# Moving layer-0 loads of a fused convolution kernel from the convolution stretches into the expansion stretches

## The chip, the cores and the metric

The program runs on one core of a Trainium2 chip. The metric is the device time of one execution in microseconds (us); for the kernel before it is the median of three runs.

A core has a tensor engine (PE; its weight loads are listed apart as PEld), a vector engine (DVE), a scalar engine (ACT), GpSimd (POOL) and a sync engine (SP). Here SP issues nearly all loads and POOL all stores. The transfers themselves run on 16 DMA engines which all issuing engines share. Each engine runs its own instructions strictly in order, and the engines wait for one another through semaphores.

## The reference, cut to what matters

Four residual layers work on x of shape (4, 64, 256, 256) in float32. The change touches layer 0 alone:

```python
# layer 0, C = 64 channels, hidden = 192, patch p = 8
v = group_norm(x)                                  # 32 groups over the whole image
v = einsum('bchw,oc->bohw', v, w_in)               # 64 -> 384 channels, "expansion"
v = irfft2(rfft2(patches 8x8 of v) * fft_filter)   # per channel, per patch
v = depthwise_conv3x3(v, w_dw)                     # padding 1
x1, x2 = split(v, 2, axis=1)
x = x + einsum('bchw,oc->bohw', gelu(x1) * x2, w_out)   # "projection"
# layer 1: x + conv3x3(group_norm(x)); layer 2: x + a thresholded convolution;
# layer 3: x + a Fourier operator with 16x16 modes
```

The filter on a patch and the 3x3 convolution together are one linear map from the pixels of a patch and its neighbours to the pixels of a patch, with other weights for each of the 384 channels. The kernel builds these maps at its start and writes them to HBM as `wts`.

## The kernel before, in words

**Blocks.** Layer 0 is cut into 12 blocks p: three for each of the 4 images, each of 11 rows of patches (`NR`), with one row more on top. In a block the hidden channels are done in four groups (`kb` = 0 to 3). For each group there is first an *expansion stretch*: `expand(p, kb, t)` for the rows t = 0 to 11 that lie in the image. PE multiplies the normalized x row `xn` with `win` (L444 for even t, L450 for odd t), and ACT and DVE copy the result from PSUM into the large tile `u` (L459, L461 to L463). Then there is a *convolution stretch*: `convolve(p, kb, g)` for g = 0 to 11, in which PE applies the maps of four channel pairs (L494, L503), ACT does the gelu (L510), DVE multiplies by the gate (L511), and POOL stores the gated planes `g` to HBM (L514).

**Projection, one block late.** The gated planes of block p-1 are read back from HBM while block p is computed. `project(p-1, r, half)` takes the pixel rows r = 0 to 7 of all patches in two halves, 16 units in a block and four in each group. PE multiplies by `w_out` (L591, L598), DVE adds to the residual rows `r` and takes statistics (L607 to L618), and POOL stores the new x (L622). Before it, `load_half` must have loaded the residual rows (`load_r`, L559, two transfers, in half 0 only) and the gated planes (`load_g`, L546 and L550, six transfers in half 0 and eight in half 1). The tiles `g1` and `g6` have two buffers each, so the load for unit (r+1, half) waits for PE to be done with unit (r, half).

**Other loads.** `load_w` brings the maps for two convolutions, three loads ahead, into four buffers (L471). `load_stats` and `next_stats` read a tenth or so of the next image in each block (`st`, L627) and take its statistics on DVE (L320). `load_x` and `normalize_x` bring the rows of x for the next block (L418) and normalize them on ACT (L256) during kb 3. `st` and x share four buffers of the pool `p_x`.

**What sets the order.** The order of the instructions of PE, DVE, ACT and SP is the order in which the Python code writes them (`tc.manual_schedule`). POOL is placed by its data alone. A transfer issued by SP has a place in SP's list, but no time: SP issues it as soon as the instructions ahead of it in that list are issued and its own waits are over. These are the wait for a free buffer, the wait for data in HBM, and the wait for one of eight completion semaphores, which the transfers of SP use in turn, so that each waits for the one eight before it.

## Time and profile before

| what | value |
|---|---|
| median of 3 runs | 6649.44 us (6638.31 to 6666.61) |
| the profiled execution | 6626.21 us |
| its span | 6624.4 us |
| PE busy in the span | 6040.5 us (91%) |
| DVE, ACT, POOL busy | 4275.7, 3238.8, 1050.4 us |
| layer 0, from the first expansion to the end of the last convolution | about 100 to 3937 us of the span |
| loads by SP in the whole program | 923.09 MB, 54.8% of the time of 16 DMA engines |
| stores by POOL | 500.14 MB, 21.7% |
| instruction fetches, queue q8 | 843 transfers, 13.81 MB |

A row of waits reads: engine and tile that waited, "<-", what ended the wait, then the sum in us, the number of waits and the longest. "issue" means that the profile shows nothing for which the engine waited. A row of a window reads: from and to in us, busy us of PE, PEld, DVE, ACT and POOL with the number of instructions, the granted clock of PE (1.00 is full), the mean busy share of the 16 DMA engines (which may exceed 1 a little, as records of neighbouring packets overlap), and GB/s. A row of the timeline reads: start, duration, engine, line, operation, tiles, and in square brackets the idle time before it with its releaser.

### The profile page before, as it was taken

To read this page: it belongs to the slowest core of one execution; us is meant where nothing else is said; L and a number is where in the kernel's file an instruction comes from. 1 tells how busy PE (TensorE), PEld (TensorE's weight loads), DVE (VectorE), ACT (ScalarE), POOL (GpSimd) and SP (SyncE) were. 2 spreads that over 40 slices of the span, in tenths; PEclk is the share of its full clock that TensorE was granted. 3 is DMA by queue.
4 is the path that set the end of the run, shared out by engine and by line. 5 is a ranking of instruction groups with operands and counts; after the bars stand their busy time and mean duration, and the time that the engine had idled before them with its cause. 6 is when DMAs were issued, how large, how long until landed. Compare 5 with 4: busy or idle time off the path is not lost.

```text
span 6624.4 us, 238282 instructions
## 1 busy us (share of the span) xinstructions
PE 6040.5 (91%) x106712; PEld 3213.7 (49%) x106712; DVE 4275.7 (65%) x5924; ACT 3238.8 (49%) x4564; POOL 1050.4 (16%) x1646
## 2 busy tenths in 40 slices
PE   2999999999999999999999986999899999999987
PEld 1455555555555555555555543333344444443576
DVE  5556555555555555555555545999798898885355
ACT  4454434344434444344444422777777887783211
POOL 3111111111111111111111111111022222221011
PEclk9999999999999999999999997999999999999855
DMA  8577777777878877877767669999666666677889
GB/s 236 152 206 211 216 213 222 218 216 213 230 213 238 219 222 207 223 214 220 210 193 206 188 194 247 232 229 228 165 177 176 168 180 173 173 187 264 318 351 394
DMA packets 878510, 1447.67 MB, mean 219 GB/s; under 512 B 77252, under 2 KB 586452, under 8 KB 875444
## 3 DMA queue, kind: packets, MB, share of 16 engines
q1 hardware_dynamic: 725284, 923.09, 54.8%
q0 software_dynamic: 148672, 500.14, 21.7%
q8 instruction: 843, 13.81, 0.9%
q10 hardware_dynamic: 3536, 9.20, 0.5%
q14 instruction: 175, 1.43, 0.1%
HBM read 932.08 MB, written 500.04 MB: 216 GB/s over the span
## 4 chain that ended last, share of the span: by engine, by line
PE 82%; DMA 6%; ACT 5%; DVE 3%; issue 3%; SPq 0%; POOL 0%; ACTq 0%; DVEq 0%; POOLq 0%
PE pc L503 18%; PE pc L494 12%; PE m L869 10%; PE psu L444 9%; PE one L1110 8%; PE div L1069 6%; PE po L591 4%; ACT u L459 4%; PE psu L450 4%; PE psz L1099 2%; PE po L598 2%; DMA x<-x 2%; PE psa L1297 2%; DMA g<-g 2%; PE psy L1444 1%
## 5 line engine op out<-in xcount | busy, mean ns | idle before, releaser
L511 DVE TENSOR_TENSOR h<-h,pc 128x374 f32<-128x374 f32 x1152 | 574.7, 541 | 1268.7 <-ACT h L510 1267.7
L510 ACT ACTIVATE h<-pc 128x374 f32<-128x374 f32 x1152 | 492.6, 480 | 1824.9 <-PE pc L503 1822.0
L503 PE MATMUL pc<-u,w 64*16 64x374 f32 (+2 forms) x27648 | 1244.1, 483 | 0.0
L494 PE MATMUL pc<-u,w 64*64 64x374 f32 x9216 | 928.6, 494 | 81.1 <-DVE u L463 32.2
L514 POOL DMA_DIRECT2D g<-h x576 | 416.7, 723 | 3111.0 <-DVE h L511 2904.7
L503 PEld LDWEIGHTS pc<-u,w 64*16 64x16 f32 (+2 forms) x27648 | 413.8, 92 | 769.5 <-issue 768.9
L444 PE MATMUL psu<-win,xn 64*128 64x96 f32 x8704 | 627.0, 283 | 131.8 <-ACT u L459 110.5
L459 DVE COPY u<-psu 64x384 f32<-64x384 f32 x1088 | 604.3, 555 | 167.7 <-PE psu L444 155.7
L459 ACT COPY u<-psu 64x384 f32<-64x384 f32 x1088 | 560.0, 515 | 238.9 <-PE psu L444 218.8
L444 PEld LDWEIGHTS psu<-win,xn 64*128 64x128 f32 x8704 | 574.0, 192 | 202.6 <-ACT u L459 143.6
L1055 DVE TENSOR_TENSOR q<-xn 128x2313 f32<-128x2313 f32 (+2 forms) x256 | 627.4, 2492 | 1.7 <-ACT xn L256 1.7
L1110 PE MATMUL one<-z,wp 32*32 32x512 f32 x16384 | 592.1, 596 | 17.8 <-issue 13.6
L494 PEld LDWEIGHTS pc<-u,w 64*64 64x64 f32 x9216 | 350.3, 133 | 531.0 <-issue 354.7
L256 ACT ACTIVATE xn<-x,nb,r 128x1024 f32<-128x1024 f32 (+3 forms) x272 | 486.8, 1793 | 244.6 <-DMA x<-x 140.8
L1056 ACT ACTIVATE q<-q 128x2313 f32<-128x2313 f32 (+2 forms) x256 | 529.0, 2086 | 32.7 <-DVE q L1055 31.2
L450 PE MATMUL psu<-win,xn 64*64 64x96 f32 x17408 | 458.2, 252 | 81.9 <-issue 57.2
L1069 PE MATMUL div<-q,ones 64*32 64x512 f32 x8192 | 466.3, 594 | 12.9 <-ACT q L1056 9.3
L1110 PEld LDWEIGHTS one<-z,wp 32*32 32x32 f32 x16384 | 367.6, 103 | 223.6 <-issue 80.1
L450 PEld LDWEIGHTS psu<-win,xn 64*64 64x64 f32 x17408 | 395.5, 137 | 126.0 <-issue 77.0
L1143 POOL DMA_DIRECT2D x<-r x512 | 275.5, 547 | 969.8 <-DVE r L1140 945.1
L591 PE MATMUL po<-g,wo 128*64 128x176 f32 (+1 forms) x3072 | 315.8, 348 | 63.3 <-DMA g<-g 41.3
L869 PE MATMUL m<-t,wk 64*64 64x512 f32 x3072 | 341.1, 588 | 0.0
(162 smaller groups left out, 6668.1 us busy)
## 6 DMA issues: line engine op xcount, KB each, us to landing
g<-h POOLq DMA_DIRECT2D x576, 374.0 KB, 7.0
x<-x SPq DMA_DIRECT2D x240, 640.0 KB, 6.4
w<-wt SPq DMA_DIRECT2D x288, 448.0 KB, 8.4
x<-x SPq DMA_DIRECT2D x100, 1024.0 KB, 14.2
g<-g SPq DMA_DIRECT2D x414, 187.0 KB, 5.7
g<-g SPq DMA_DIRECT2D x736, 93.5 KB, 6.0
x<-in_x_dram SPq DMA_DIRECT2D x256, 256.0 KB, 8.1
x<-o POOLq DMA_DIRECT2D x128, 512.0 KB, 8.2
```

The source lines that it names most:

```text
L444: nc.tensor.matmul(ps[s][:, k, at], xn[halves[s], n : n + 2].rearrange("p n r w -> p (n r w)"), win[halves[s], kb, 0 : 2 * PB], start=True ...
L450: nc.tensor.matmul(ps[s][halves[1 - odd], k, at], xn[halves[s], n + odd].rearrange("p r w -> p (r w)"), win[halves[s], kb, PB * (1 - odd) ...
L459: copy(at(h, 8 * s + o), v[k, c : c + PB])
L494: nc.tensor.matmul(out(C * c, C, k, h), w[halves[h], k, 2 * (G % 2) + c, 0:C], cells(h, 4 * g + 2 * k + c, 0, 0), start=True, stop=False, ...
L503: nc.tensor.matmul(out(q, m, k, h), w[halves[h], k, 2 * (G % 2) + c, c0 : c0 + m], cells(h, 4 * g + 2 * k + c, down, right), start=False, ...
L511: nc.vector.tensor_mul(h[:, k], h[:, k], ps[k][:, 1, 0:L])
L591: nc.tensor.matmul(out(k, s, x), wo1, moving(g1[:, 2 * k], 2 * half + k, s, x), start=(x == 0), stop=False, skip_group_check=True,)
L869: nc.tensor.matmul(rows2(m)[halves[j], s], w[dx][halves[s]], ts[n][halves[s], i, 2 * j : 2 * j + 2, dx : dx + W], start=(dx == 0), stop=(d ...
L1055: nc.vector.tensor_sub(d, p0, p1)
L1056: nc.scalar.activation(d, d, AF.Square)
L1069: ins = nc.tensor.matmul(ps[quarters[j], h], ones[halves[h]], q[n, g, k][halves[h], r + 2 * j : r + 2 * j + 2, o : o + W], start=(m == 0), ...
L1110: ins = nc.tensor.matmul(rows2(ps[g])[quarters[j], k], w[quarters[i]], z[quarters[i], h, 2 * j + dy : 2 * j + dy + 2, dx : dx + W], tile_p ...
```

## The change

Three things are done, all in layer 0.

1. The maps are stored in HBM, and held in the tile `w`, with the two halves k of a channel next to each other. A load of `w` then reads one run of 3584 bytes per partition, where it read two of 1792 bytes.
2. `unit` (projection and the next load) stands at g = 0, 3, 6, 9, where it stood at 1, 4, 7, 10. The loads that follow the projections at g = 6 and 9, and the first two of a block, are kept in a list `later` and written at t = 7 and t = 9 of the next expansion stretch.
3. The statistics parts (kb 0 to 2) and the first four x rows of the next block (kb 3) are written at t = 8, 9, 10 and 11 of the expansion stretch. They stood at g = 0, 3, 6, 9, and at g = 11 of kb 2. `next_stats` runs at the odd g.

```diff
-        wts = [dr.tile([2, 64, 2, Q, NC], F32, name=f"wt{t}") for t in range(HID // C)]
+        wts = [dr.tile([2, 64, Q, 2, NC], F32, name=f"wt{t}") for t in range(HID // C)]
...
-            w = wl[j] = p_w.tile([128, 2, 4, NC], F32, tag="w", name=f"w_{j}")
+            w = wl[j] = p_w.tile([128, 4, 2, NC], F32, tag="w", name=f"w_{j}")
             nc.sync.dma_start(
-                w, wts[k // 8][:, :, :, 4 * (k % 8) : 4 * (k % 8) + 4].rearrange("h i k c n -> (h i) k c n")
+                w, wts[k // 8][:, :, 4 * (k % 8) : 4 * (k % 8) + 4].rearrange("h i c k n -> (h i) c k n")
             )
...
             for p in range(NB + 1):
-                ahead = 1
+                ahead, later = 1, []
...
                 for r in range(ahead):
                     for half in range(2):
-                        load_half(p - 1, r, half)
-
-                def unit():
+                        later.append((p - 1, r, half))
+                        if p == NB:
+                            load_half(*later.pop())
+
+                def unit(wait=False):
                     at = next(units, None)
                     if at:
                         project(p - 1, *at)
-                        load_half(p - 1, at[0] + ahead, at[1])
+                        later.append((p - 1, at[0] + ahead, at[1]))
+                        if not wait:
+                            load_half(*later.pop(0))
...
                     for t in range(NR + 1):
                         if 0 <= i0 + t < NP:
                             expand(p, kb, t)
+                        if t in (7, 9) and later:
+                            load_half(*later.pop(0))
+                        if t >= 8:
+                            if kb == 3 and t - 8 < len(fresh):
+                                load_x(fresh[t - 8])
+                            elif kb < 3 and nk:
+                                loaded.append(nk.pop(0))
+                                load_stats(b + 1, loaded[-1])
...
-                        if g in (1, 4, 7, 10):
-                            unit()
+                        if g in (0, 3, 6, 9):
+                            unit(wait=g > 3)
                         if kb < 3:
-                            if g % 3 == 0:
-                                if len(loaded) == 2 or not nk:
-                                    for k in loaded[: 1 if nk else 2]:
-                                        next_stats(b + 1, loaded.pop(0))
-                                if nk:
-                                    k = nk.pop(0)
-                                    load_stats(b + 1, k)
-                                    loaded.append(k)
-                            if kb == 2 and g == NG - 1:
-                                for row in fresh[:4]:
-                                    load_x(row)
+                            if g % 2 and loaded:
+                                next_stats(b + 1, loaded.pop(0))
```

The remaining lines of the diff give the matmuls of `convolve` and the stores of `weights` the new order of the indices. The numbers of instructions on PE, DVE and SP don't change.

More of the change, by code (lines that the diff above doesn't have):

```diff
@@ L395, in weights @@
                             nc.gpsimd.dma_start(
-                                wts[t][h, 32 * hh : 32 * hh + 32, k, :, n0 : n0 + n].rearrange("i c n -> c i n"),
+                                wts[t][h, 32 * hh : 32 * hh + 32, :, k, n0 : n0 + n].rearrange("i c n -> c i n"),
                                 T[quarters[2 * h + k], :, :, c0 : c0 + n].rearrange("p a b n -> p (a b) n"),
@@ L494, in convolve @@
                         nc.tensor.matmul(
-                            out(C * c, C, k, h), w[halves[h], k, 2 * (G % 2) + c, 0:C], cells(h, 4 * g + 2 * k + c, 0, 0),
+                            out(C * c, C, k, h), w[halves[h], 2 * (G % 2) + c, k, 0:C], cells(h, 4 * g + 2 * k + c, 0, 0),
                             start=True, stop=False, tile_position=(h * C, c * C), skip_group_check=True,
@@ L503, in convolve @@
                             nc.tensor.matmul(
-                                out(q, m, k, h), w[halves[h], k, 2 * (G % 2) + c, c0 : c0 + m],
+                                out(q, m, k, h), w[halves[h], 2 * (G % 2) + c, k, c0 : c0 + m],
                                 cells(h, 4 * g + 2 * k + c, down, right),
```

## The prediction

> **What bounds the kernel now.** I read the page first. Its busy row and its slices put PE at 91% of the span, and at 90% or more in nearly every slice of layer 0 (slices 1 to 23), while the 16 DMA engines are busy 70 to 80% there.
>
> ```profile
> span 6624.4 us, 238282 instructions
> ...
> PE 6040.5 (91%) x106712; PEld 3213.7 (49%) x106712; DVE 4275.7 (65%) x5924; ACT 3238.8 (49%) x4564; POOL 1050.4 (16%) x1646
> ...
> PE   2999999999999999999999986999899999999987
> ...
> DMA  8577777777878877877767669999666666677889
> ```
>
> So a transfer matters only where PE ends up waiting. I asked for PE's waits from 300 to 3700 us:
>
> ```profile
> PE psu L444 <- ACT u L459: 94.3, 145, 1.5
> PE psu L450 <- issue: 57.2, 48, 4.2
> PE pc L494 <- DVE u L463: 29.3, 29, 1.3
> ...
> PE psu L444 <- issue: 18.7, 23, 1.8
> ...
> PE po L591 <- DVE h L511: 0.3, 1, 0.3
> ```
>
> No wait here ends with a landing of g, w, st or x (the 41.3 us of `po` waiting for g in the whole program lie in the drain after layer 0). The rest is eviction of `psu`, and 76 us of "issue", all in the expansion stretches. I took those apart in the timeline:
>
> ```profile
> 1700.59 0.40 PE L450 MATMUL psu<-win,xn 64*64 64x96 f32 x8 [2.28 <-issue]
> ```
>
> In the DMA records an instruction fetch of q8 runs from 1698.29 to 1699.34, and PE goes on 1.25 us later. The other long gaps from 1525 to 1720 us look alike: a fetch ends at 1530.34, the gap at 1531.55; 1626.38 and 1627.79. There are 843 fetches for 215,917 PE and PEld instructions: one per 256. A fetch starts late when SP has transfers in flight: by my count 1.8 us after the earliest point with none in flight, 4.5 us with six. An expansion stretch uses 256 instructions in 5.8 us (192 per pair of rows of 4.4 us), a convolution stretch in 7.1 us (128 per 3.53 us), so only the former starves. The windows show which stretches are loaded (first and second half of an expansion, of the convolution after it, then an expansion of kb 3):
>
> ```profile
> 1525.90:1540.10 14.20, 12.53 (x295) 11.50 (x288) 10.41 (x19) 9.61 (x19) 0.72 (x1) 0.88 0.87 277
> 1540.10:1554.20 14.10, 11.43 (x289) 10.29 (x289) 12.08 (x23) 11.34 (x23) 0.00 (x0) 1.00 0.30 53
> 1554.20:1581.30 27.10, 26.14 (x412) 10.94 (x420) 12.03 (x22) 5.75 (x13) 3.63 (x5) 0.94 0.54 143
> 1581.30:1608.30 27.00, 27.00 (x498) 11.39 (x482) 15.48 (x27) 5.14 (x12) 7.27 (x10) 1.00 1.05 292
> ...
> 1608.30:1622.70 14.40, 12.63 (x312) 11.62 (x310) 12.14 (x23) 11.36 (x23) 0.72 (x1) 1.00 1.02 286
> 1622.70:1637.20 14.50, 12.07 (x273) 10.91 (x271) 10.55 (x19) 9.51 (x19) 0.00 (x0) 0.88 0.85 146
> ```
>
> The DMA engines are full in the second half of the convolution and spill into the first half of the expansion; in kb 3 the x rows fill the second half too. Clock 0.88 is a stretch at half clock just after a stall.
>
> Measured from the timeline, an undisturbed expansion takes 23.6 us (first block of an image), 26.4 or 26.2 us (second, third). Above that, over blocks 1 to 11, stand 10.1 us in kb 0, 20.0 in kb 1, 15.1 in kb 2 and 32.0 in kb 3: 77 us. Convolution stretches have 31 us above their quiet lengths (52.5, 51.7, 53.3 us), mostly 1.6 us at their head at half clock. These 108 us (1.6%) are all that the placing of transfers can give back.
>
> **The Trainium skill.** "Runtime: NRT & Kernel Launch", Instruction fetch mechanics, says that instructions stream in blocks of 16 KiB (256 instructions) over the sequencer's own DMA queue and calls the cost mostly hidden. The block size agrees (13.81 MB in 843); hidden it is not, by 76 us. "DMA: Bandwidth & Descriptors", Issuing engines are not separate DMA queues, says all issuers share 16 engines; the late fetches agree. Its section Why small descriptors are slow gives about 3 cycles per packet besides 32 bytes a cycle. "TensorE: Matmul & The Clock Gate", What's actually happening, says that PE falls to half clock after an idle window of about 3.4 us. Here half clock lasts 3 to 7 us, but after gaps of only 1 to 2 us.
>
> **The change part by part.** *Weight runs.* 288 loads take 128 packets in place of 256. A 1792-byte packet takes 75 ns in the median; 3584 bytes are not in the trace, 4096 take 159 to 189, so no gain per byte shows. By the skill's price it is 59 against 57.5 cycles, 2.5% of 12% of DMA time. Nobody waits for w: 0 us. The weights lie in the same partitions in runs of 64 columns, so loads into PE cost the same.
>
> *Projections at g = 0, 3, 6, 9.* The same instructions, 2.05 us of PE each. At g = 3 a half-1 unit and `next_stats` now meet on DVE: 0.8 + 0.8 (L610, L612) + 1.8 (L618) + 1.3 (L320) = 4.7 us before the next L511. That convolution and its gelu end 3.5 + 0.5 us after the projection, so its gate is 0.7 us late; its banks are next needed some 3 us after that. Hidden, 0 us; without this slack it would be 0.7 us × 44 = 31 us.
>
> *Moved loads.* SP has no clock, and it already runs ahead of its place:
>
> ```profile
> 1379.73 1.31 SPq L559 DMA_DIRECT2D r<-in_x_dram  x2
> 1399.09 0.48 SPq L546 DMA_DIRECT2D g<-g  x1
> ```
>
> These are residual and planes of one `load_half`: the residual went out 19 us before the projection it is written behind. What holds SP back in layer 0 is the buffer of g:
>
> ```profile
> SPq L546 <- PE po L591: 1178.8, 108, 32.5
> ```
>
> In the changed list the load at t = 7 has its buffer free since g = 6, the statistics parts since g = 1 to 7, the load at t = 9 since g = 9. The last thing that holds them is the weight load at g = 10, which needs convolution 9 done. So they leave some 9 us before the expansion begins, not in its second half. The volume until SP is held again (by the projection at g = 0): residual 704 KB, planes 1122, part 512, planes 1122, three parts 1536, w 448, next residual 704: 6148 KB or 6.3 MB, in 27 transfers. In 9 us of the convolution some 180 GB/s are free (290 less 374 KB of g per 3.53 us): 1.6 MB. That leaves 4.7 MB, 16 us at 290 GB/s, in the expansion. Before it was, by the windows, 14.2 × 277 + 14.1 × 53 = 4.7 MB in kb 2, 14.4 × 286 + 14.5 × 146 = 6.2 in kb 3, and 7.1 in kb 0 (13.8 us at 302 and 13.8 at 210 GB/s). After: 4.7 in kb 1, 4.2 in kb 2 (three parts), 4.7 in kb 3. In kb 0 the planes must wait for the last store of g, some 8 us into the stretch, as before (SP stood there 6.4 us): 6.6 MB. Sum of the four: 22.7 to 20.2 MB, 11% less. Stalls in proportion: 77 × 0.11 = -8 us. The full second half of the convolution gets lighter; its own excess of 31 us is tied to the clock and may give back 4. Sum: **-12 us**.
>
> Who waits behind SP? The weight load of g = 0 is queued behind the 5 MB and needed at g = 6, some 25 us later; the planes of t = 7 land some 10 us into the expansion and are needed at its end plus 5.6 us; x row 0 of kb 3 has 15 us to spare. If that cover were gone, PE or ACT would stand a landing of 8 us (r, w, x: 7.9 to 8.4 us) per stretch.
>
> The profiled execution (6626.2) lies 23 us under the median of the runs, so I subtract from both: 6614 for a profile like this one, **6637 us** for the median.
>
> **Rivals.** *A, slower: every expansion becomes like kb 3.* From the start SP keeps eight transfers in flight, without the pauses that the wait for g gave it, and fetches starve longer. For it: kb 3, where this is so now, has 32.0 / 11 = 2.9 us of excess, and 6.9 at worst. Against: kb 1 is as full in its first half. It decides once 6 MB instead of 4.7 fall inside a stretch. Price: kb 0 to 2 go from 45 to 96 us: +51 us, 6700 us.
>
> *B, faster: fetches stop starving.* Blocks 9 and 10, which load no statistics, show it: their kb 1 and 2 have 0.1 us of excess at 0.83 to 0.95 in the first half. If the lighter convolution lets the expansion start with empty queues, some 60% of 77 us and 8 of the 31 go: -54 us, 6595 us. Against: SP runs ahead.
>
> *C, the change doesn't do what it says, and only shuffles stalls.* That is my own case in its flattest form: 6649 ± 15 us.
>
> **How the numbers follow.** Half a per cent, 33 us, is about what a measurement of this kernel can tell from no change. My case with C: 0.55, from -30 to +20 us. A: 0.26, from +20 to +70. B: 0.19, from -30 to -75. About a fifth of A lies within 33 us and a tenth of B. So faster 0.17, same 0.62, slower 0.21. The range 6600 to 6700 us leaves out half of B and half of A, about 0.2.
>
> **What would show it.** Right: planes and parts issued from some 9 us before an expansion; DMA share in the second half of the convolution down from 1.05 to about 0.7, up from 0.54 in its first half; first half of the expansion still near 1.0, second half below 0.4 in kb 1 and 2; "issue" before L450 and L444 60 to 80 us; no new wait of PE or ACT for a landing. Wrong: "issue" above 110 us (A) or under 35 us (B), loads held until the second half by a wait I overlooked, or `pc` waiting for DVE after g = 3.

## The result, and the profile after

The changed kernel takes 6674.27 us in the median (6647.1 to 6705.01), the kernel before 6650.26 us (6630.05 to 6677.6) beside it: ratio 1.0039, 95% interval 1.0021 to 1.0057. It is a little slower, where I had forecast a gain of 0.2%. The profiled execution took 6683.42 us.

The page of the changed kernel, the same rows as before:

```profile
span 6681.6 us, 238181 instructions
...
PE 6076.7 (91%) x106712; PEld 3230.2 (48%) x106712; DVE 4275.3 (64%) x5924; ACT 3241.8 (49%) x4564; POOL 1045.1 (16%) x1646
...
PE   2999999999999999999999986999899999999988
...
DMA  8477878787878777877867759999666667667889
```

PE has the same number of matmuls and 36 us more of busy time. That is not more work. By the clock records, layer 0 has 198 us at half clock, 123 before, and matmuls at half clock are busy for longer. The two traces exaggerate the change: the profiled execution before lies 24 us under its median, the one after 9 us above, so that they are 57 us apart and the medians 24. Half clock in particular scatters: three kernels of this study with the time of the kernel before (`weights_only`, `dose`, `hold_only`) have 174, 184 and 201 us of it. Layers 1 to 3 take 2687 us before and 2692 after, so 52 of the 57 us between the two profiled executions lie in layer 0. From the timeline its expansion stretches went from 1318 to 1362 us in sum, its convolution stretches from 2518 to 2526.

PE's waits from 300 to 3700 us, after:

```profile
PE psu L444 <- ACT u L459: 91.3, 138, 0.8
PE psu L450 <- issue: 74.9, 55, 3.5
PE pc L494 <- DVE u L463: 28.9, 29, 1.3
PE psu L444 <- issue: 24.7, 20, 2.4
...
PE pc L494 <- DMA st<-in_x_dram: 2.0, 1, 2.0
```

"Issue" grew from 75.9 to 99.6 us; all else stands as it stood, and one wait that the profile ends with a landing is 2 us in the whole layer. So the loss is the old stall, late instruction fetches, and more of it. It is clear of the scatter: the kernel before and the three with its time have 68 to 84 us of "issue" here, the changed one 100. The windows of a block (kb 2: two halves of the expansion, two of the convolution; then the expansion of kb 3), with the columns of the prediction's windows:

```profile
1550.80:1564.30 13.50, 11.46 (x300) 10.57 (x294) 11.23 (x21) 10.62 (x21) 0.72 (x1) 1.00 1.02 324
1564.30:1577.80 13.50, 11.25 (x287) 10.20 (x287) 11.38 (x21) 10.36 (x22) 0.00 (x0) 1.00 0.60 120
1577.80:1604.00 26.20, 25.24 (x432) 11.10 (x440) 13.35 (x24) 5.77 (x13) 4.36 (x6) 1.00 0.57 167
1604.00:1630.10 26.10, 26.10 (x479) 10.94 (x456) 11.54 (x20) 5.14 (x12) 6.53 (x9) 1.00 0.77 228
1630.10:1645.20 15.10, 11.36 (x298) 10.37 (x292) 11.02 (x21) 10.14 (x21) 0.72 (x1) 1.00 0.96 274
1645.20:1660.30 15.10, 11.00 (x290) 10.21 (x292) 11.66 (x21) 10.78 (x21) 0.00 (x0) 1.00 0.88 163
```

The second half of the convolution is lighter as forecast (1.05 to 0.77). But the expansion of kb 2 now carries 13.5 × 324 + 13.5 × 120 = 6.0 MB where I had reckoned with 4.2, that of kb 3 6.6 where I had 4.7. Over blocks 1 to 11 the four expansions of a block carry 24.2 MB in the mean, against 19.9 before: the change put 22% more into them, and I had forecast 11% less. SP's timeline just before and in that expansion, which starts at 1550.8, shows how the loads came there:

```profile
1534.92 7.36 SPq L471 DMA_DIRECT2D w<-wt  x2
1542.45 1.32 SPq L559 DMA_DIRECT2D r<-in_x_dram  x2
1543.81 0.64 SPq L546 DMA_DIRECT2D g<-g  x1
...
1549.27 3.00 SPq L627 DMA_DIRECT2D st<-in_x_dram  x2
1553.27 0.45 SPq L546 DMA_DIRECT2D g<-g  x1
...
1560.65 2.39 SPq L627 DMA_DIRECT2D st<-in_x_dram  x4
```

The residual, written at t = 7, leaves 8.3 us before the expansion starts, and the last of the statistics parts, written at t = 8 to 10, are issued by 1563.0, in the first half. The change says "second half"; SP, which has nothing to wait for there, does it in the tail of the convolution and the first half.

### The profile page after: what moved, and what is told of

It is laid out like the page before. It is cut to its first block, busy times and chain, and to the rows that moved or that the text cites. A ratio compares the mean times of both kernels' runs of the same rounds, so it can differ in the third digit from the quotient of the medians.

```text
span 6681.6 us, 238181 instructions
## 1 busy us (share of the span) xinstructions
PE 6076.7 (91%) x106712; PEld 3230.2 (48%) x106712; DVE 4275.3 (64%) x5924; ACT 3241.8 (49%) x4564; POOL 1045.1 (16%) x1646
## 4 chain that ended last, share of the span: by engine, by line
PE 83%; DMA 5%; ACT 5%; issue 3%; DVE 3%; SPq 0%; POOL 0%; ACTq 0%; DVEq 0%; POOLq 0%
PE pc L503 18%; PE pc L494 13%; PE m L872 10%; PE psu L444 9%; PE one L1113 9%; PE div L1072 7%; ACT u L459 4%; PE po L591 4%; PE psu L450 3%; PE po L598 2%; DMA x<-x 2%; PE psz L1102 2%; DMA g<-g 2%; PE psa L1300 2%; PE psy L1447 1%
## 5 line engine op out<-in xcount | busy, mean ns | idle before, releaser
L511 DVE TENSOR_TENSOR h<-h,pc 128x374 f32<-128x374 f32 x1152 | 574.8, 541 | 1273.5 <-ACT h L510 1273.3
L450 PE MATMUL psu<-win,xn 64*64 64x96 f32 x17408 | 473.2, 256 | 110.7 <-issue 81.0
```

The lines of the kernel that those rows point to most:

```text
L450: nc.tensor.matmul(ps[s][halves[1 - odd], k, at], xn[halves[s], n + odd].rearrange("p r w -> p (r w)"), win[halves[s], kb, PB * (1 - odd) ...
L511: nc.vector.tensor_mul(h[:, k], h[:, k], ps[k][:, 1, 0:L])
```

## What a late fetch costs: a table from all traces

An expansion of some 1,100 PE and PEld instructions meets four or five block boundaries, and at each one fetch (q8) brings the next 256. For every fetch I took its delay after the earliest point, as in the prediction, and the "issue" gap of PE that follows within 2 us of its end. The earliest point is a place in PE's own stream of instructions: hardly any fetch number k (from 0) starts before PE and PEld instruction 256k + 165 or so (1.5% of them do). Over the traces of the 20 kernels of this study, blocks 1 to 11 (number of fetches; share followed by a gap; mean gap in us):

```
delay of the fetch   first half of expansion   second half        convolution
under 3 us           775  0.00  0.00           886  0.00  0.00    3034  0.00  0.00
3 to 4 us            422  0.24  0.14           308  0.10  0.07    1218  0.00  0.00
4 to 5 us            376  0.53  0.51           311  0.16  0.17    1192  0.00  0.00
5 to 6 us            227  0.75  1.08           193  0.45  0.61     571  0.01  0.01
6 to 7 us             79  0.81  1.38           134  0.58  1.10     147  0.22  0.12
over 7 us             28  0.89  2.16           108  0.69  1.90      49  0.27  0.25
```

This is what the prediction lacked. In these traces a delay under 3 us costs nothing anywhere; in the first half of the expansion half of the delays of 4 to 5 us already stop PE, in the convolution it takes over 6 us. The delay goes with the number of SP's transfers that are in flight at the earliest point: in the mean of all traces 1.3 us with none, 2.5 with two, 3.1 with four, 4.2 with six and 4.4 with eight. (All eight completion semaphores are counted here, each transfer until the last landing before its semaphore's next use. The prediction's "4.5 us with six" seems to leave out two of them: without these two my count also gives 4.5 us at six, which was then the most that it could show.) What counts is therefore less how much is moved during a stretch than whether many transfers are in flight at the moment of an early fetch. By fetch, in the order in which they come in an expansion (mean delay / sum of the gaps behind it over blocks 1 to 11, us):

```
kb 1 and 2      1st        2nd        3rd        4th        5th
before          4.2/3.5    4.6/19.7   3.4/0.6    2.0/0.0    3.0/0.0
after           4.7/8.8    4.6/8.5    5.1/23.6   3.5/0.6    2.7/0.0
units_only      4.5/11.0   5.1/25.6   3.4/0.0    1.9/0.0    3.1/0.0
stats_only      3.4/3.5    4.6/21.4   5.4/22.0   3.1/0.0    2.7/0.0
stats_hold      2.6/0.0    2.2/1.6    1.8/0.0    1.8/0.0    4.4/0.0
dose            3.9/3.0    2.5/0.3    2.9/2.3    5.7/17.6   4.9/0.0
hold_only       3.9/1.3    2.4/0.0    3.7/15.8   3.3/0.2    3.0/0.0
held_3          1.0/0.0    1.2/0.0    1.9/0.0    4.2/7.9    6.2/0.4
paced_s         2.2/0.0    3.1/1.3    2.8/0.0    2.0/0.0    4.2/0.9
```

Before, most of the gaps stood behind the second fetch; after, most stand behind the third, and fewer behind the second. (Where exactly the earliest point is set moves a few us between neighbouring cells; the sum of a row stays.) The fifth may be over 6 us late for nothing: what it brings runs in the convolution. One profiled execution scatters: the expansions of the kernel with only the new weights have 92 us of excess in its profile against 77 before, at the same time. So times below are judged by their ratios, and the traces for what waited on what. "Excess" is as in the prediction, over blocks 1 to 11.

If the volume were the measure, the excess would follow the megabytes. These are all packets of the DMA records that fall into the 44 expansions of blocks 1 to 11, loads, stores and fetches (the kernels are described below):

```
              MB in the expansions   excess there, us   ratio of times
before        219                     77                1
after         266                    113                1.0039
units_only    200                    117                1.0051
stats_only    225                    111                1.0069
dose          253                     87                0.9994
paced_3       217                     28                0.9989
paced_3r      215                     54                0.9956
stats_hold    190                     58                0.9956
held_3        147                     48                0.9970
```

With about the volume of before, or a little less, the excess is anything from 28 to 117 us.

The times go with PE's "issue" waits. From 300 to 3700 us these are 89 to 100 us in five kernels at 1.004 to 1.007 (`after`, `planes_late`, `stats_only`, `units_only`, `stats_x_only`), 68 to 84 in the four within 0.001 of the kernel before, and 27 to 50 in eight at 0.994 to 0.999. Three stand apart: `units_hold` and `held` have 58 and 29 us at 1.005 and 1.006, and lose their time elsewhere, as will be seen; `planes_only` has 88 at 0.998, but its profiled execution took 36 us more than its median.

## Experiments

**The parts alone.** `weights_only` has only the new order of the weights; `units_only` only the new places of the projections (with the loads that follow them); `planes_only` both, and the loads behind the last two projections (planes and residual) deferred to t = 7 and 9; `stats_x_only` only the statistics parts and x rows moved.

```diff
# units_only
-                        if g in (1, 4, 7, 10):
+                        if g in (0, 3, 6, 9):
# stats_x_only, beside next_stats at odd g
+                        if t >= 8:
+                            if kb == 3 and t - 8 < len(fresh):
+                                load_x(fresh[t - 8])
+                            elif kb < 3 and nk:
+                                loaded.append(nk.pop(0))
+                                load_stats(b + 1, loaded[-1])
```

> The kernel before with the runs of 3584 bytes alone. Theory F (the changed kernel loses its 0.39% because more of SP's transfers fall into the expansion stretches and delay PE's instruction fetches there): nothing that falls into an expansion is changed, ratio to before 0.999 to 1.001, excess of the expansions over their quiet length 77 us as before (65 to 90). Rival W (longer packets hold the DMA engines longer, so fetches wait longer): ratio 1.002 to 1.004, excess near 113 us as in the changed kernel.

> The kernel before with the projections and the loads behind them at g = 0, 3, 6, 9, statistics and x as before. Theory F: the last planes of a group leave 3.5 us earlier in the convolution, so less of them spills into the expansion: ratio 0.997 to 1.000, excess 55 to 80 us. Rival U (the new place of the projections costs by itself, through banks of PSUM or through DVE at g = 3): ratio 1.002 to 1.005, with the convolution stretches 20 to 40 us longer in sum and the expansions unchanged.

> The changed kernel with statistics parts and x rows as before: only the planes and residuals of two units per group are moved. Theory F: the expansion gets the moved planes in one burst, and the part of g = 9 still spills into it, so most of the loss is here: ratio 1.001 to 1.004, excess 85 to 115 us, kb 1 above 25 us. If the statistics parts make the loss: ratio 0.998 to 1.000, excess under 75 us.

> The kernel before with statistics parts and x rows alone at t = 8 to 11 of the expansion, planes as before. Theory F: 2 MB more fall into every expansion beside the planes that spill over: ratio 1.001 to 1.004, excess 90 to 120 us, kb 1 and 2 above 25 us each. If only the planes matter: ratio 0.998 to 1.001, excess 65 to 85 us.

```
weights_only   0.9995 [0.9979, 1.0012]
units_only     1.0051 [1.0032, 1.0069]
planes_only    0.9980 [0.9967, 0.9993]
stats_x_only   1.0070 [1.0043, 1.0096]
```

The weights are worth nothing, as reckoned. The projections' move costs 0.5% and the statistics parts and x rows 0.7%, which I had both at or below zero. Deferring the planes gives back the projections' share and 0.2% more. The small sum of the change is made of parts larger than itself. For `units_only` the time is the one that I had given to the rival, but not the place: its convolutions have 49 us of excess (34 before), its expansions 117 (77).

**Projections and planes.** `planes_late` is `planes_only` with the projections at g = 1, 4, 7, 10. `units_hold` has the projections at 0, 3, 6, 9 and each load behind them held, by a dependency on the last matmul, until the convolution g + 1 is done.

```diff
# planes_late against planes_only
-                        if g in (0, 3, 6, 9):
-                            unit(wait=g > 3)
+                        if g in (1, 4, 7, 10):
+                            unit(wait=g > 4)
# units_hold
...
+            d = (queue or nc.sync).dma_start(out, src)
+            if held[0]:
+                self.after(d, last[0])
```

> The weight layout and the deferred planes of the change, with the projections left at g = 1, 4, 7, 10 and the statistics parts and x rows loaded where they were before. If the parts of the change add up (projections moved +0.5%, planes deferred -0.7%, weights 0), this kernel is at 0.993 of the time before (0.990 to 0.996, some 6600 us), and its gain is in the expansions of kb 1 to 3 and in the second half of the convolution. Rival: deferring the planes only repaid what moving the projections had cost, so that without the move it is worth nothing: 0.998 to 1.001.

> The kernel before with the projections moved to g = 0, 3, 6, 9, but each projection's loads held until the convolution after it is done, so that the transfers leave when they left before. If the move costs because the loads leave 3.5 us earlier: 0.998 to 1.002. If it costs because of where the projections stand on PE and DVE: 1.004 to 1.007, as with the loads moved along (1.0051), with excess in the expansions of 105 to 120 us.

`planes_late` measured 1.0047 [1.0031, 1.0063], not 0.993: the parts do not add up. Without the earlier projections the deferred planes cost 0.5%, with them they gain; behind the second fetch of kb 1 and 2 stand 30.2 us of gaps in `planes_late` and 14.7 in `planes_only`. The same transfers leave 3.5 us later there; that they then meet another fetch is a reading, not shown by a run of its own.

`units_hold` measured 1.0052 [1.0038, 1.0066], as if the place on PE and DVE were to blame. Its trace says otherwise: "issue" in the expansions of blocks 1 to 11 fell from 94 us in `units_only` to 56, below the 76 of before, so holding the loads did take stalls away. The time went to a new place. The convolutions of kb 3 have 65 us of excess, 9 in `units_only`, and PE's waits have a row that is in neither of the two:

```profile
PE pc L501 <- DVE h L518: 32.3, 10, 4.4
```

**Loads held to their rows, and paced.** `held` is the changed kernel with every load that is written into the loop over t held until its row is expanded. `paced` has the projections at 1, 4, 7, 10, statistics parts as before, planes and residual of the last two projections in small groups at t = 1, 2, 4, 6, 8, x rows of kb 3 at t = 3, 5, 7, 9, all held; in the convolution the planes go ahead of the residual.

```diff
# paced
+                        held[0] = True
+                        if t in (1, 2, 6) and later:
...
+                        if t in (2, 4, 6, 8):
+                            n = (len(todo) + 1) // 2 if t in (2, 6) else len(todo)
+                            for job in todo[:n]:
+                                load(*job)
+                            del todo[:n]
```

> The changed kernel, with every load that it moved into the loop over t held until the expansion of its row t is done, so that SP can no longer run ahead of its place. If what costs is that SP starts the loads some 8 us before an expansion and keeps eight in flight through its first half: first half of the expansion near empty, excess in the expansions 66 to 90 us, 0.998 to 1.002 of the time before. If what costs is the volume that falls inside an expansion, whenever it leaves: the same 6 MB or more fall in the second half and in the head of the convolution, excess 110 to 140 us, 1.004 to 1.010.

> Projections at g = 1, 4, 7, 10, statistics parts loaded as before, and the planes and the residual of the last two projections loaded a few at a time, each group held until row t = 1, 2, 4, 6 or 8 of the expansion is done, the x rows of kb 3 at t = 3, 5, 7, 9; new weight layout. If the number of transfers in flight is what makes fetches late: three or four in flight in an expansion in place of six to eight, excess below 45 us, issue below 50 us, 0.986 to 0.992 of the time before. If only the volume counts: as with the planes deferred in bursts, 0.992 to 0.996. If the stalls are tied to neither: 0.998 to 1.004.

`held` 1.0058 [1.0045, 1.0072], `paced` 0.9980 [0.9970, 0.9990]: neither time is the one that I had forecast for fetches delayed by transfers in flight. `held` lies in the range that I had given to the volume, but its expansions have 29 us of excess in sum, not 110 to 140; and the stalls there did go in both. Excess in the expansions of kb 0 to 2: 45 us before, 24 in `held`, 12 in `paced`, where 2.8 of SP's transfers are in flight in the first half of kb 1 and 2 in place of 5.8. But the convolutions of kb 3 have 103 and 59 us of excess (11 before), by the same kind of wait (`held`):

```profile
PE pc L501 <- DVE h L518: 44.6, 19, 5.4
```

ACT's waits for x are 191 us in `held` and 149 in `paced`, 63 before. ACT normalizes the x rows of the next block in kb 3, strictly in order with the gelus; a row that lands late holds up the next gelu, then DVE's product, then PE. A wait that cost nothing at 63 us does at 149.

**What made the x rows late.** `paced_3` keeps kb 3 as before but for the order of planes and residual; `paced_u` is `paced_3` with the projections at 0, 3, 6, 9; `paced_3r` and `paced_ur` are the two with the residual ahead of the planes again in kb 3.

```diff
# paced_3 against paced: no x rows at t, and the burst at g = 11 of kb 2 back
-                            unit(wait=g > 4)
+                            unit(wait=g > 4 and kb != 2)
# paced_u against paced_3
-                        if g in (1, 4, 7, 10):
-                            unit(wait=g > 4 and kb != 2)
+                        if g in (0, 3, 6, 9):
+                            unit(wait=g > 3 and kb != 2)
# paced_3r against paced_3 (the calls of kb 2 and 3 have early=True)
+                if half == 0 and early:
+                    load_r(p, r)
                 for job in load_g(p, r, half):
                     load(*job)
-                if half == 0:
+                if half == 0 and not early:
                     load_r(p, r)
```

> The paced kernel with its pacing kept to kb 0 to 2: in kb 3 planes, residual and x rows are loaded where the kernel before loads them. Projections at g = 1, 4, 7, 10. If the 48 us that the paced kernel lost in the convolutions of kb 3 came from the x rows, which were late for ACT there: convolution excess back to about 30 us, expansions of kb 0 to 2 together below 20 us of excess, kb 3 about 32, and 0.991 to 0.994 of the time before. If pacing only moves stalls about: 0.997 to 1.001.

> The same as paced_3, with the projections at g = 0, 3, 6, 9. If moving the projections costs only through loads that then fall into the expansions, it costs nothing where these are paced: within 0.002 of paced_3. If it costs by their place on PE and DVE: 0.004 to 0.006 above paced_3.

> paced_3 (projections at g = 1, 4, 7, 10) with the residual again ahead of the planes from kb 2's second half on, as in the kernel before. If the 57 us that the convolutions of kb 3 lost came from the residual, which left behind the planes and pushed the x rows: convolution excess of kb 3 below 20 us, ACT waits for x below 90 us, expansions of kb 3 back to about 30 us, 0.992 to 0.995 of the time before. If not: 0.998 to 1.000 as paced_3.

> The same with the projections at g = 0, 3, 6, 9. If their place is free by itself, and paced_u beat paced_3 only through x rows that were less late: within 0.002 of paced_3r, 0.992 to 0.996. If their place is worth something in itself, as paced_u against paced_3 (0.9952 against 0.9989): 0.003 or more below paced_3r.

```
            time                        excess in us: convolutions of kb 3 / ACT's waits for x
paced_3     0.9989 [0.9975, 1.0004]     57 / 143
paced_u     0.9952 [0.9938, 0.9966]     21 /  65
paced_3r    0.9956 [0.9945, 0.9966]     14 /  56
paced_ur    0.9968 [0.9956, 0.9981]     14 /  19
```

The timeline of ACT in `paced_3`, in kb 3 of a block, and of PE behind it:

```profile
1664.54 0.86 ACT L517 ACTIVATE h<-pc 128x374 f32<-128x374 f32 x2 [1.51 <-PE pc L510]
1672.36 1.24 ACT L256 ACTIVATE xn<-x,nb,r 128x1024 f32<-128x1024 f32 x1 [6.97 <-DMA x<-in_x_dram]
1673.51 0.83 ACT L517 ACTIVATE h<-pc 128x374 f32<-128x374 f32 x2
```

```profile
1674.60 1.59 PE L601 MATMUL po<-g,wo 128*64 128x176 f32 x16 [3.07 <-DVE h L518]
```

One x row 7 us late, one gelu after it, 3 us of PE. In that block SP issued the residual at 1637.9, 14 us into the convolution and behind the planes, with the x rows next in the list; in `paced_3r` (second fence) it left at 1615.7, 16 us before the convolution began:

```profile
1634.45 3.23 SPq L434 DMA_DIRECT2D g<-g  x6
1637.85 1.32 SPq L434 DMA_DIRECT2D r<-in_x_dram  x2
1639.27 4.58 SPq L434 DMA_DIRECT2D x<-in_x_dram  x2
```

```profile
1615.67 2.05 SPq L434 DMA_DIRECT2D r<-in_x_dram  x2
1642.24 3.28 SPq L434 DMA_DIRECT2D g<-g  x6
1645.62 1.31 SPq L434 DMA_DIRECT2D x<-in_x_dram  x2
```

Putting the two loads back into their old order takes 87 us off ACT's waits, and 0.33% off the time. `paced_ur` lies 0.12% above `paced_3r`, with overlapping intervals: where transfers no longer fall on the early fetches, the place of the projections costs nothing that can be told. `paced_u` had looked as if it gained 0.4%; that goes with the x rows, for which ACT waits 65 us there and 143 in `paced_3`.

**A dose of transfers that nobody waits for.** `dose` is the kernel before with 1.6 MB of spare transfers after t = 4 in kb 1 and 2. `hold_only` has one of 32 KB in their place, so that only the hold of SP at t = 4 remains.

```diff
# dose
+                        if t == 4 and kb in (1, 2) and p:
+                            for i in range(6):
+                                spare = p_g.tile([C, P, HW2], F32, tag=f"spare{i}", name=f"spare_{p}_{kb}_{i}")
+                                d = nc.sync.dma_start(spare, a["x"][b, :, P * i : P * i + P, 0:HW2])
+                                self.after(d, last[0])
# hold_only: in place of the six
+                            d = nc.sync.dma_start(spare, a["x"][b, :, 0:1, 0:HW2])
+                            self.after(d, last[0])
```

> The kernel before, with six extra transfers of 256 KB that nobody waits for (input rows copied into spare memory) started by SP after row t = 4 of every expansion of kb 1 and 2, where the kernel before has hardly anything in flight in the second half. It computes the same result. If transfers in flight make PE's instruction fetches late and the late fetches stop PE: fetch latency in that half from 1.8 and 2.9 us to 4 or more, excess in the expansions of kb 1 and 2 from 35 us to 60 to 90 us, nothing new in kb 0 and 3, 1.004 to 1.008 of the time before. If the stalls come from the work that the moved transfers feed, or from the clock alone: 0.998 to 1.001.

> The dose kernel with its six spare transfers cut to one of 32 KB: what remains is the hold, SP cannot run past row t = 4 of the expansions of kb 1 and 2. By the fetches of the dose kernel the hold took away some 20 us of stalls at the first two fetches of an expansion and the spare transfers added 17 us at the fourth. If so: 0.994 to 0.998 of the time before, stalls at the fourth fetch of kb 1 and 2 near 0. If neither did anything: 0.998 to 1.001, with stalls in kb 1 and 2 of 20 us or more as before.

`dose` 0.9994 [0.9982, 1.0006], `hold_only` 1.0004 [0.9995, 1.0014]. Both times lie in the range of the rival, 0.998 to 1.001; what speaks for the fetches here is the traces alone. In the table of fetches the dose does what it should at its place: the fourth fetch is 5.7 us late instead of 2.0, and 17.6 us of gaps stand behind it where there were none, though no work depends on these transfers. That is the cleanest sign that transfers in flight, not the data they bring, stop PE, by making its fetches late. The hold emptied the second fetch (19.7 to 0.3 us). The sum is nil: against `hold_only`, some 35 MB more in these 22 expansions cost nothing in time. I then expected the hold without the dose to gain; it moved the weight load and the residual that SP had sent early onto the third fetch (0.6 to 15.8 us), and gained nothing.

**The statistics parts, free and held.** `stats_only` moves only the parts to t = 8 to 10, with `next_stats` at the odd g (x rows stay). `stats_hold` is the same with each part held until its row is expanded.

```diff
# stats_hold against stats_only
-                nc.sync.dma_start(t[halves[s]], src_t[b, :, j, s])
+                d = nc.sync.dma_start(t[halves[s]], src_t[b, :, j, s])
+                if last[0]:
+                    self.after(d, last[0])
```

> The kernel before with only the statistics parts moved, as in the changed kernel, to rows t = 8 to 10; x rows, projections, planes and weights as before. If the 0.7% of statistics parts and x rows together come from the parts (1.5 MB more in the expansions of kb 0 to 2): 1.004 to 1.008. If from the x rows, which now come on top of everything else in kb 3: 0.999 to 1.002.

> Only the statistics parts moved, as in stats_only, and each held until the row t = 8 to 10 behind which it is written is expanded, so that it really is loaded in the last part of the expansion. If the parts cost (1.0069) because SP starts them far ahead of their place, into the first half: 0.997 to 1.001, with stalls at the third fetch of kb 1 back near 0. If they cost by their volume, wherever in or around the expansion: 1.004 to 1.008.

`stats_only` 1.0069 [1.0052, 1.0087], `stats_hold` 0.9956 [0.9943, 0.9969]: the same loads in the same place of the program, 1.1% apart. The timeline of SP in `stats_only`, in an expansion from 1476.9 to 1507.5, that of PE with its gaps there, and the windows of its two halves:

```profile
1480.08 6.13 SPq L627 DMA_DIRECT2D st<-in_x_dram  x8
```

```profile
1492.47 0.69 PE L444 MATMUL psu<-win,xn 64*128 64x96 f32 x8 [0.69 <-issue]
1500.45 2.00 PE L450 MATMUL psu<-win,xn 64*64 64x96 f32 x43 [2.17 <-issue]
```

```profile
1476.90:1492.20 15.30, 12.86 (x315) 11.80 (x312) 12.67 (x23) 11.66 (x23) 0.72 (x1) 1.00 0.99 271
1492.20:1507.50 15.30, 11.27 (x265) 10.20 (x265) 9.94 (x18) 9.30 (x19) 0.00 (x0) 0.89 0.37 62
```

The same expansion in `stats_hold`, from 1432.6 to 1458.95, which has no such gap: SP, then the windows of its two halves.

```profile
1434.42 1.21 SPq L551 DMA_DIRECT2D g<-g  x1
1452.43 7.08 SPq L628 DMA_DIRECT2D st<-in_x_dram  x8
```

```profile
1432.60:1445.80 13.20, 11.17 (x297) 10.30 (x290) 10.98 (x20) 10.33 (x21) 0.72 (x1) 1.00 0.44 146
1445.80:1458.95 13.15, 11.32 (x289) 10.38 (x289) 11.50 (x22) 10.63 (x22) 0.00 (x0) 1.00 0.38 98
```

Free, the eight parts leave 3 us into the stretch, right behind the planes, and keep SP's transfers going until the third fetch. Held, they leave 20 us into it and spill into the convolution, whose fetches can be late: its first half is at a DMA share of 0.80 in kb 1 (0.59 before), and the convolutions have 29 us of excess in sum (34 before). The hold does more than place the parts: the weight load and the residual that stand behind them in SP's list leave late as well (1459.6 and 1461.3 here, 1486.3 and 1487.0 in `stats_only`, still inside the stretch). So the expansions of kb 1 and 2 carry 3.2 MB in the mean, less than the 4.2 of before, and 2.4 transfers are in flight in their first half in place of 5.8. `stats_x_only` equals `stats_only`, so the x rows' part in it cannot be told from nil. In block 0, which has no planes to load, the four expansions take 117.0 us before, 126.1 in `stats_only` and 116.5 in `stats_hold`.

**The change as it was meant.** `held_3` is `held` with kb 3 as before. `paced_s` is `paced_3r` with the held parts of `stats_hold`.

```diff
# held_3 against held
-                        if t >= 8:
-                            if kb == 3 and t - 8 < len(fresh):
-                                load_x(fresh[t - 8])
-                            elif kb < 3 and nk:
-                                loaded.append(nk.pop(0))
-                                load_stats(b + 1, loaded[-1])
+                        if t >= 8 and kb < 3 and nk:
+                            loaded.append(nk.pop(0))
+                            load_stats(b + 1, loaded[-1])
...
-                            unit(wait=g > 3)
+                            unit(wait=g > 3 and kb != 2)
...
+                            if kb == 2 and g == NG - 1:
+                                for row in fresh[:4]:
+                                    load_x(row)
# paced_s against paced_3r, beside next_stats at odd g
+                        if t >= 8 and kb < 3 and nk:
+                            loaded.append(nk.pop(0))
+                            load_stats(b + 1, loaded[-1])
```

> The changed kernel (projections at g = 0, 3, 6, 9, planes at t = 7 and 9, statistics parts at t = 8 to 10, new weight layout) with two edits: every load written into the loop over t is held until its row is expanded, and kb 3 keeps the planes and x rows of the kernel before. If the change lost its time because SP ran ahead with these loads, and the held kernel because of late x rows in kb 3: excess in the expansions of kb 1 and 2 below 10 us, convolutions of kb 3 below 25 us, 0.994 to 0.998 of the time before. If loading 5 MB from row 7 on is too much wherever it is started: 1.000 to 1.005, with the loss in the convolutions of kb 0 to 2.

> paced_3r with the statistics parts moved to t = 8 to 10 as in stats_hold, held to their rows. If the two gains (0.9956 each) add up: 0.991 to 0.993. If both take away the same stalls, those of kb 0 to 2 in the first half of the expansion, and what is left is kb 3 with its 30 to 40 us: 0.994 to 0.997.

`held_3` 0.9970 [0.9958, 0.9981]: with its loads really behind row 7, and kb 3 left alone, the change is a gain. But it does not fill the expansions: in kb 1 and 2 they carry 2.7 MB (4.2 before), nothing of SP's is in flight in their first half, the second half is at a DMA share of 0.68 (0.13 before), and most of what was to be moved out of the convolution lands in its first half, which is at 1.03 (0.57). `paced_s` 0.9940 [0.9922, 0.9958], 6611.71 us against 6648.19 beside it, has the lowest ratio of the study, though its interval overlaps those of `stats_hold` and `paced_3r`: the gains mostly overlap, as the second expectation had it, since the same stalls of kb 0 to 2 can go only once. PE's waits in `paced_s`:

```profile
PE psu L451 <- ACT u L466: 114.2, 178, 0.9
...
PE psu L451 <- issue: 19.4, 9, 3.0
PE psu L457 <- issue: 15.3, 16, 3.0
```

"Issue" is 35 us instead of 76, 27 of it in kb 3, whose x rows still fill the expansion. PE's wait for the eviction of `psu` grew from 94 to 114 us; probably some of the gaps had hidden such waits.

## Why the prediction was wrong, point by point

- **What bounds the kernel: right.** Little but "issue" changed in PE's waits, and the fetches of `dose` show that transfers in flight cause it. That "only the former starves" is right within a little: the convolution's fetches have to be over 6 us late.
- **Weight runs, 0 us: right** (0.9995). The packets of SP's loads fell by 36,864, as 288 × 128 says; one of 3584 bytes took 142 ns in the median, two of 1792 take 150, and no time followed.
- **Projections, "hidden, 0 us": wrong by 0.5%.** The term on DVE and PSUM was right: `units_only` shows no wait of `pc` for L511, and `paced_ur` against `paced_3r` finds the place free. What I did not price is the loads that SP issues behind each projection, which leave 3.5 us earlier with it; with them held, in `units_hold`, the gaps in the expansions fall below those of before, though not the time. Why these 3.5 us made it worse in `units_only` and better in `planes_only` against `planes_late` is not settled: the expansions of `units_only` carry less than before (200 MB against 219, and some 4.8 of SP's transfers in flight in the first half of kb 1 and 2 against 5.8), its first two fetches are later all the same.
- **SP runs ahead, "so they leave some 9 us before the expansion begins": right** (8.3 us).
- **The volume, "22.7 to 20.2 MB": the step that failed, and it gave the forecast its wrong sign.** What falls into the four expansions of a block went up by 22% (19.9 to 24.2 MB in the mean of blocks 1 to 11), not down by 11%; in the block that the prediction had taken apart, 22.3 to 25.7. By the prediction's own rule that is 77 × 0.22 = +17 us in place of -8. By the windows, kb 2, 3 and 0 have 6.0, 6.6 and 6.4 MB where I had 4.2, 4.7 and 6.6. In the 8.4 us before the expansion of kb 2 the engines moved 2.0 MB in all, of which some 0.9 were stores of g (374 KB per 3.53 us): 1.1 MB of loads, where I had 1.6, and the weight load that SP had issued just before the residual is among them. I also left out the stores of g that land in the expansion itself. By estimate these terms, 0.5, 0.5 and 0.8 MB, account for nearly all of the 1.8 that kb 2 has too much.
- **"Stalls in proportion": the second failure, in the size.** The excess rose by 36 us, not 17, and megabytes in an expansion are no measure of its stalls. Against `hold_only`, `dose` has 1.6 MB more in each of 22 expansions and costs nothing; `paced_3` has the volume of before and 28 us of excess in place of 77; `stats_only` has 3% more than before and loses 0.7%, where `stats_hold`, with the same parts 17 us later in the stretch and SP's next loads behind them, gains 0.4%. The better measure is the number in flight at the first three fetches. In the first half of kb 1 and 2 it went from 5.8 to 7.5 with the change.
- **The convolution gives back 4 us: no.** Its second half went from a share of 1.02 to 0.76 in kb 0 to 2, its excess from 34 to 41 us (the prediction had counted 31). The convolution never suffered from full DMA engines, so relieving it was worth nothing: its fetches, late as they are, stop PE for some 2 us a trace in the mean. That the change moves load from a stretch that bears it to one that doesn't was in my own numbers (7.1 us against 5.8 per 256 instructions), and I did not draw the conclusion.
- **Rival A was nearest.** Its threshold, 6 MB in a stretch, was reached and its sign is right. Its price of 51 us for kb 0 to 2 was too high: their excess went from 45 to 75 us, and the medians are 24 us apart. In this trace kb 1 became like kb 3 (44 us of excess), kb 2 did not (20). Rival B's premise, that a lighter convolution lets expansions start with empty queues, failed on SP's run-ahead, as I had noted against it; where the loads are held it comes about in part.
- **The signs to watch:** early issue, first half near 1.0, lighter convolution: seen. Second half below 0.4: 0.55 and 0.50. "Issue" between 60 and 80: 99.6, short of the 110 that I had set for A.

## What to carry to other kernels

A load's place in an issuing engine's list tells what it stands behind, not when it leaves: to place a load in time, give it something to wait for, and look at what stands behind it in the list (here x rows for ACT). When PE stalls on instruction fetches, find which fetch of which stretch is late and keep few transfers in flight at that moment; a stretch with few instructions per microsecond is the place for traffic. When a schedule change moves a per cent or less, measure its parts alone: here +0.5, -0.7 and +0.7% stood behind +0.4, and they hang on one another: deferring the planes gains 0.7% after the projections are moved and loses 0.5% without.

## What was not expected of the hardware

- Fetches of 16 KiB, which take 0.9 to 1.4 us each, start 1.3 us after the earliest point with no SP transfer in flight, and 4.4 us after with eight (means over all 20 traces). PE tolerates about 3 us in this code's densest stretch.
- Gaps of 1 to 2 us can be followed by matmuls at half clock for some us. "TensorE: Matmul & The Clock Gate" in the Trainium skill, What's actually happening, speaks of an idle window of about 3.4 us. Over blocks 1 to 11 of all traces, half clock follows within 7 us on 25 of 305 issue gaps under 0.7 us, on 90 of 220 from 1.2 to 2 us, and on 156 of 208 of 2 us or more.
- Transfers from HBM to HBM delay fetches as loads into SBUF do (`dose`: 2.0 to 5.7 us at the fourth fetch).
